# Two attention layers on one core: four key tiles per divisors' matmul, normalizations moved to ScalarE, elementwise work off GpSimd

## The chip, the cores and the metric

The kernel runs on one core of a Trainium2 chip. A core has five engines that work side by side and meet through semaphores: TensorE (matrix multiplication), VectorE and ScalarE (elementwise work), GpSimd (here elementwise work and the issue of some transfers) and SyncE (the issue of the other transfers). The metric is the device time of one execution in microseconds. The kernel before takes 3778.3 us, the median of three runs (3777.52 to 3778.91).

## The reference

The input `x` is four images of 256 channels and 64 x 64 pixels, all in fp32. Two layers follow each other, each of them `x = x + layer(groupnorm(x))` with 32 groups of 8 channels.

```python
# layer 0 ("A"): 8 heads of 32; queries from 4096 pixels, keys and values from a 2x2 strided convolution (1024)
q = einsum(Wq, x);  k = conv2x2(x, Wk);  v = conv2x2(x, Wv)
attn = softmax((q.k + q.(rel_h + rel_w)) * scale)        # 4096 x 1024 for each image and head
out = attn . v
# layer 1 ("B"): the 4096 pixels cut into 4 areas of 1024; attention inside each area
q, k, v = conv1x1(x, w_qkv) + b_qkv
attn = softmax(q.k * scale)                              # 1024 x 1024 for each image, area and head
out = attn . v + depthwise_conv7x7(v)
out = conv1x1(out, w_proj) + b_proj
```

In both layers each image has 8 chunks of 512 queries and two groups of four heads. The kernel calls one chunk with one group of four heads a **unit**: 16 units make a **block** (one layer of one image), and the eight blocks run in the order A0, A1, B0, A2, B1, A3, B2, B3 (layer and image). A unit goes over its 1024 keys in 8 **steps** of 128 keys.

## The kernel before

A unit's step `j` computes scores for four heads, exponentiates them without subtracting a maximum (a check at the end sends inputs with too large sums down another path), and multiplies the weights `p` of the step before with the values. `p` is a pair of tiles of 128 x 2 x 512, two heads each.

```python
def scores(unit, j):
    q, k = unit[1](), unit[2]()
    p = [pool.tile([P, 2, CH], FP, tag="p", name="p", bufs=10) for _ in range(2)]
    pairs = [ps_pair("s"), ps_pair("s")]
    for h in range(4):
        rows = slice(HD * h, HD * h + HD)
        T.matmul(pairs[h // 2][:, h % 2, :], lhsT=k[rows, j * P : (j + 1) * P], rhs=q[rows, :], ...)   # L213
    for i in range(2):
        S.activation(p[i], pairs[i], AF.Exp, scale=SCALE)                                              # L218
    return p

def weighted(unit, j, p, av):                        # av += v^T p, four matmuls, L225
    ...
```

The softmax's denominators are sums of `p` over all keys. They are made by a matmul with ones, and to halve those, the weights of two steps are added first: the first pair of heads by a transfer that accumulates (issued from GpSimd), the second by VectorE.

```python
def add_up(p, q):
    G.dma_start(p[0], q[0], accum_op=ALU.add)                                                          # L232
    V.tensor_add(p[1], p[1], q[1])                                                                     # L233

def divisors(g, n, p):
    ...
    for h in range(4):
        T.matmul(dens[g][HD * h : HD * h + HD, :], lhsT=ones[:, :HD],
                 rhs=p[h // 2][:, h % 2, :], start=(n == 0), stop=(n == NKT // 2 - 1))                 # L242
```

After a unit's last divisors, `divide` copies them to SBUF (L254), sends them through DRAM to spread them over the partitions, takes reciprocals (L259), broadcasts these back (`rb`) and multiplies (L266). The main loop, with the plan of side work in `do(g, j)`:

```python
while step < last or plan or later:
    g, j = divmod(step, NKT)
    if step < last:
        p = scores(units[g], j)
    do(g, j)
    if before is not None:
        weighted(*before)
        if j == 0:
            avs[g - 1] = pool.tile([P, CH], FP, tag="av", name="av_sb", bufs=2)
            S.copy(avs[g - 1], before[3])                                                              # L639
    if step < last:
        if j == 0:
            av = psum.tile([P, CH], FP, tag="av", name="av", bufs=1)
        if j % 2:
            add_up(before[2], p)
            later[step + 3] = g, j // 2, before[2]
    before = (units[g], j, p, av) if step < last else None
    if step in later:
        g, n, p = later.pop(step)
        divisors(g, n, p)
        if n == NKT // 2 - 1:
            divide(g, units[g])
    step += 1
```

The side work is placed by unit and step: projections for the next blocks (each a group of long matmuls with a copy on ScalarE), the normalizations

```python
def normalize(key, dst, src, t):
    mean, rstd = norms[key]
    V.tensor_scalar(dst, src, mean[:, t : t + 1], rstd[:, t : t + 1], ALU.subtract, ALU.mult)          # L194
```

of `taps` (256 elements a call, 128 calls), `hq` (512, 64 calls), `hv` (512, 64 calls) and `h` (1024, 32 calls), the residual adds on GpSimd (`add_residual`, L380, and `add_conv`, L484, each 32 times 128 x 1024), and the depthwise convolution, 49 taps for each of 32 pieces, on VectorE:

```python
            V.scalar_tensor_tensor(dst, src, w, dst, ALU.mult, ALU.add)                                # L578
    ...
    pace = 3.2                                 # units for one piece of the convolution
    start = max(start, ends[b] + 4.5)          # so it runs from about unit 20.5 to unit 126 of 128
```

Every engine works through its instructions in the order in which the program gives them.

Of the kernel before, what the change touches and what calls it, by code (L numbers as in the profile page):

```python
# [48 lines left out]
def direct_path(  # L49
# [109 lines left out]
    def plan_norm(key, g, j):  # L159
# [4 lines left out]
        def aggregate():  # L164
            for tag, cols in (("mv", 2), ("gmean", 1), ("dev", 1), ("gvar", 1), ("rstd", 1)):
                shape = [P, CT, cols] if cols > 1 else [P, CT]
                made[tag] = pool.tile(shape, FP, tag=tag, name=f"{tag}_{name}", bufs=3)
            norms[key] = made["gmean"], made["rstd"]
# [13 lines left out]
        def variances():  # L182
# [3 lines left out]
            G.tensor_tensor(made["rstd"], made["gvar"], neghalf, ALU.pow)  # L186

# [4 lines left out]
    def normalize(key, dst, src, t):  # L192
        mean, rstd = norms[key]
        V.tensor_scalar(dst, src, mean[:, t : t + 1], rstd[:, t : t + 1], ALU.subtract, ALU.mult)  # L194
# [12 lines left out]
    def scores(unit, j):  # L207
        q, k = unit[1](), unit[2]()
        p = [pool.tile([P, 2, CH], FP, tag="p", name="p", bufs=10) for _ in range(2)]
# [20 lines left out]
    def add_up(p, q):  # L230

        G.dma_start(p[0], q[0], accum_op=ALU.add)  # L232
        V.tensor_add(p[1], p[1], q[1])  # L233
# [3 lines left out]
    def divisors(g, n, p):  # L237
# [3 lines left out]
        for h in range(4):  # L241
            T.matmul(  # L242
                dens[g][HD * h : HD * h + HD, :], lhsT=ones[:, :HD],
                rhs=p[h // 2][:, h % 2, :], start=(n == 0), stop=(n == NKT // 2 - 1),
            )

    def divide(g, unit):
# [20 lines left out]
        at(g + 1, 6, reciprocals)  # L268
        at(g + 2, 1, multiply)

    def att_of(key):
        if key not in atts:
            atts[key] = pool.tile([P, CT, CH], FP, tag="att", name="att_" + "_".join(map(str, key)), bufs=2)
# [3 lines left out]
    def plan_a(b, u, prep):  # L277
# [101 lines left out]
        def add_residual(c):  # L379
            G.tensor_tensor(xcs[c], xcs[c], atts["A", b, c], ALU.add)  # L380
# [7 lines left out]
        for c in range(NCH):  # L388
# [4 lines left out]
            at(g + 2, 2, lambda c=c: load_residual(c))  # L393
            at(g + 3, 2, lambda c=c: add_residual(c))
            at(g + 3, 4, lambda c=c: store_chunk(c))
# [12 lines left out]
    def plan_b(b, u):  # L408
# [74 lines left out]
        def add_conv(c):  # L483
            G.tensor_tensor(rest[c][0], rest[c][0], atts["B", b, c], ALU.add)  # L484
# [18 lines left out]
        for c in range(NCH):  # L503
            g = u + 2 * c
            at(g + 2, 5, lambda c=c: load_rest(c))
            at(g + 3, 2, lambda c=c: add_conv(c))
            at(g + 3, 5, lambda c=c: project(c))
            at(g + 3, 7, lambda c=c: finish(c))
# [89 lines left out]
    for i, (layer, b) in enumerate(BLOCKS):  # L598
        u = i * UNITS
        if layer == "A":  # L600
            units += plan_a(b, u, u - UNITS)
            ends[b] = u + UNITS
            plan_norm(("B", b), u + UNITS + 1, 5)
# [4 lines left out]
    for b in range(B):  # L608
        start = max(start, ends[b] + 4.5)
# [20 lines left out]
    while step < last or plan or later:  # L630
# [9 lines left out]
        if step < last:  # L640
            if j == 0:
                av = psum.tile([P, CH], FP, tag="av", name="av", bufs=1)
            if j % 2:

                add_up(before[2], p)
                later[step + 3] = g, j // 2, before[2]
        before = (units[g], j, p, av) if step < last else None
        if step in later:
            g, n, p = later.pop(step)
            divisors(g, n, p)  # L650
# [609 lines left out]
```

## Time and profile before

| | us |
|---|---|
| device time, median of 3 | 3778.3 |
| span of the profiled execution | 3771.5 |
| TensorE matmuls busy | 3622.4 |
| VectorE busy | 2966.1 |
| ScalarE busy | 2365.4 |
| GpSimd busy | 639.7 |
| accumulating transfers, share of 16 engines' span | 38.2% |
| all other transfers of the SyncE queue, same measure | 21.1% |

A row of the profile's groups has the line of the kernel, the engine, the operation, the tiles it writes and reads with their shapes, the count, then the busy time in us and the mean length of one in ns, then the idle time of the engine just ahead of these instructions and what ended it. A matmul's end is modelled, so that neighbouring matmuls overlap in it. fp32 matmuls stand as two records each. In the timeline each row has the start in us, the length in us of the merged instructions, the engine, the line, the tiles and the count.

### The profile page before, as it was taken

Reading aid. Unit: us, or ns where it says so; the run is one execution under the profiler, and the core shown is the slowest. Engines: PE = TensorE matmul, PEld = TensorE weight load, DVE = VectorE, ACT = ScalarE, POOL = GpSimd, SP = SyncE. Lnnn points to the kernel's source line nnn. Section 1 sums busy time; section 2 is a strip of 40 time slices with the busy share of each in tenths; the row PEclk is TensorE's granted clock in tenths of the full one; section 3 lists DMA queues with packets and bytes.
Section 4 is the critical chain, followed back from the end, with each engine's and each line's share of the span. In section 5 each row is a group of like instructions: output and inputs, shape, how many; then the busy total and the mean of one; then the engine's idle time right before and its main releaser. Section 6 shows DMA issues by size and latency. Waiting matters only on the chain.

```text
span 3771.5 us, 57900 instructions
## 1 busy us (share of the span) xinstructions
PE 3622.4 (96%) x23330; PEld 1204.1 (32%) x23330; DVE 2966.1 (79%) x2972; ACT 2365.4 (63%) x2673; POOL 639.7 (17%) x600
## 2 busy tenths in 40 slices
PE   6999999999999999999999999999999999999996
PEld 5223432223332343222333234322233333333321
DVE  2333235999998878999998887899994689899992
ACT  1777466666666555666666665566666666666664
POOL 0122111111111111111111111111111111111111
PEclk9999999999999999999999999999999999999998
DMA  4666456666755655666675565566566556565554
GB/s 155 152 139 158 111 129 148 157 148 150 184 128 117 173 127 136 143 149 150 145 168 136 141 156 130 125 154 138 139 142 156 122 130 161 130 159 127 120 133 114
DMA packets 238790, 535.38 MB, mean 142 GB/s; under 512 B 62945, under 2 KB 69345, under 8 KB 238513
## 3 DMA queue, kind: packets, MB, share of 16 engines
q0 software_dynamic: 74080, 269.57, 38.2%
q1 hardware_dynamic: 163072, 259.61, 21.1%
q8 instruction: 184, 3.01, 0.3%
q10 hardware_dynamic: 1360, 2.43, 0.2%
q14 instruction: 94, 0.76, 0.1%
HBM read 193.85 MB, written 69.21 MB: 70 GB/s over the span
## 4 chain that ended last, share of the span: by engine, by line
PE 77%; DVE 11%; DMA 8%; issue 3%; ACT 1%; SPq 0%; POOL 0%; DVEq 0%; ACTq 0%; POOLq 0%
PE s L213 24%; PE av L225 20%; PE den L242 10%; DMA p<-p 6%; DVE acc L578 6%; PE k0ps L316 3%; PE v0ps L334 3%; PE ops L491 3%; PE v1ps L442 3%; PE k1ps L426 3%; PE vals_ps L538 3%; PE q1ps L453 3%; DVE p L233 2%; PE q0ps L370 2%; ACT p L218 1%
## 5 line engine op out<-in xcount | busy, mean ns | idle before, releaser
L218 ACT ACTIVATE p<-s 128x1024 f32<-128x1024 f32 x2048 | 1990.7, 1022 | 872.0 <-PE s L213 601.9
L578 DVE SCALAR_TENSOR_TENSOR acc<-vin,wpe_sb,acc 128x976 f32<-128x976 f32 (+14 forms) x1536 | 1950.4, 1270 | 35.2
L233 DVE TENSOR_TENSOR p<-p 128x1024 f32<-128x1024 f32 x512 | 633.0, 1236 | 577.3 <-PE av L225 271.0
L232 POOL DMA_DIRECT2D p<-p x512 | 440.3, 860 | 2930.0 <-ACT p L218 1133.1
L242 PE MATMUL den<-p,ones 128*32 128x512 f32 x4096 | 574.8, 599 | 73.4 <-DMA p<-p 61.7
L213 PE MATMUL s<-q,k_A 32*128 32x512 f32 x4096 | 626.9, 645 | 0.3 <-ACT p L218 0.3
L213 PE MATMUL s<-q,k_B 32*128 32x512 f32 x4096 | 615.0, 646 | 0.0
L225 PE MATMUL av<-p,v_B 128*32 128x512 f32 x4096 | 549.7, 608 | 0.4 <-ACT av_sb L639 0.3
L225 PE MATMUL av<-p,v_A 128*32 128x512 f32 x4096 | 548.5, 608 | 1.1 <-ACT av_sb L639 0.8
L213 PEld LDWEIGHTS s<-q,k_A 32*128 32x128 f32 x4096 | 197.9, 184 | 434.3 <-issue 219.2
L213 PEld LDWEIGHTS s<-q,k_B 32*128 32x128 f32 x4096 | 186.2, 184 | 435.1 <-issue 155.9
L242 PEld LDWEIGHTS den<-p,ones 128*32 128x32 f32 x4096 | 134.2, 110 | 422.2 <-issue 268.3
L225 PEld LDWEIGHTS av<-p,v_A 128*32 128x32 f32 x4096 | 80.8, 108 | 382.0 <-issue 342.7
L225 PEld LDWEIGHTS av<-p,v_B 128*32 128x32 f32 x4096 | 80.9, 108 | 363.2 <-issue 346.7
L491 PE MATMUL ops<-cv,wp_sb 128*128 128x512 f32 x256 | 119.9, 611 | 14.9 <-POOL cv L484 14.7
L538 PE MATMUL vals_ps<-hv,wqkv_sb 128*128 128x512 f32 x256 | 117.4, 607 | 7.7 <-ACT p L218 7.7
L316 PE MATMUL k0ps<-taps,wk_sb 128*128 128x256 f32 x512 | 119.6, 388 | 3.0 <-DVE taps L194 3.0
L442 PE MATMUL v1ps<-wqkv_sb,h 128*128 128x256 f32 x512 | 119.1, 386 | 0.0
L453 PE MATMUL q1ps<-h,wqkv_sb 128*128 128x512 f32 x256 | 118.4, 605 | 0.0
L426 PE MATMUL k1ps<-h,wqkv_sb 128*128 128x512 f32 x256 | 118.4, 605 | 0.0
L370 PE MATMUL q0ps<-hq,wq_sb 128*128 128x512 f32 x256 | 118.3, 605 | 0.0
L334 PE MATMUL v0ps<-wv_sb,taps 128*128 128x256 f32 x512 | 117.2, 383 | 0.0
(79 smaller groups left out, 1632.3 us busy)
## 6 DMA issues: line engine op xcount, KB each, us to landing
p<-p POOLq DMA_DIRECT2D x512, 512.0 KB, 5.2
rb<-recs SPq DMA_DIRECT2D x512, 64.0 KB
xs<-in_x SPq DMA_DIRECT2D x32, 512.0 KB
xa<-in_x SPq DMA_DIRECT2D x32, 512.0 KB
hq<-in_x SPq DMA_DIRECT2D x32, 512.0 KB
xc<-in_x SPq DMA_DIRECT2D x32, 512.0 KB
xmid<-xc SPq DMA_DIRECT2D x32, 512.0 KB
hv<-xmid SPq DMA_DIRECT2D x32, 512.0 KB
```

Source lines behind the costliest of these rows:

```text
L213: T.matmul(pairs[h // 2][:, h % 2, :], lhsT=k[rows, j * P : (j + 1) * P], rhs=q[rows, :], start=True, stop=True,)
L218: S.activation(p[i], pairs[i], AF.Exp, scale=SCALE)
L225: T.matmul(av[HD * h : HD * h + HD, :], lhsT=v[:, j, unit[0] * P + HD * h : unit[0] * P + HD * h + HD], rhs=p[h // 2][:, h % 2, :], start= ...
L232: G.dma_start(p[0], q[0], accum_op=ALU.add)
L233: V.tensor_add(p[1], p[1], q[1])
L242: T.matmul(dens[g][HD * h : HD * h + HD, :], lhsT=ones[:, :HD], rhs=p[h // 2][:, h % 2, :], start=(n == 0), stop=(n == NKT // 2 - 1),)
L316: T.matmul(ps, lhsT=wk0_sb[:, t, 2 * i + w, qd * P : (qd + 1) * P], rhs=taps[a][:, t, i, w], start=(n == 0), stop=(n == 7),)
L426: T.matmul(ps[:, half, :], lhsT=wqkv_sb[:, t, 1, qd * P : (qd + 1) * P], rhs=hs[a][:, t, half * CH : (half + 1) * CH], start=(t == 0), sto ...
L442: T.matmul(ps[:, m, :], lhsT=hs[a][:, t, kt * P : (kt + 1) * P], rhs=wqkv_sb[:, t, 2, :], start=(t == 0), stop=(t == CT - 1),)
L453: T.matmul(ps[:, qd, :], lhsT=wqkv_sb[:, t, 0, qd * P : (qd + 1) * P], rhs=hs[c // 2][:, t, (c % 2) * CH : (c % 2 + 1) * CH], start=(t == ...
L491: T.matmul(ps[:, to, :], lhsT=wp_sb[:, t, to * P : (to + 1) * P], rhs=cv[:, t, :], start=(t == 0), stop=(t == CT - 1),)
L578: V.scalar_tensor_tensor(dst, src, w, dst, ALU.mult, ALU.add)
```

## The change

Four steps' weights, not two, are added up before one group of divisors' matmuls, which halves the number of those groups from 512 to 256. For that, VectorE adds the second pair's tiles three times in four steps, and the transfers of the first pair form a small tree: steps 1 into 0 and 3 into 2, and three steps later 2 into 0. The weights stay longer, so there are 13 buffers of `p` for 10, and one buffer of `att` for two. The divisors now stand in steps 1 and 5, after the weighted sum; before, they stood in every even step.

VectorE hands the normalizations to ScalarE, as one activation with a scale and a shift per channel (`shift = -mean * rstd`, made by two small operations on GpSimd), and takes over the residual adds from GpSimd, which is left with issuing transfers, apart from these small operations. The other edits move side work to fit: reciprocals, multiplications, residual adds and projections later, the convolution 0.4 unit later.

```diff
--- before.py
+++ after.py
@@ -162,10 +162,10 @@
         made = {}
 
         def aggregate():
-            for tag, cols in (("mv", 2), ("gmean", 1), ("dev", 1), ("gvar", 1), ("rstd", 1)):
+            for tag, cols in (("mv", 2), ("gmean", 1), ("dev", 1), ("gvar", 1), ("rstd", 1), ("shift", 1)):
                 shape = [P, CT, cols] if cols > 1 else [P, CT]
                 made[tag] = pool.tile(shape, FP, tag=tag, name=f"{tag}_{name}", bufs=3)
-            norms[key] = made["gmean"], made["rstd"]
+            norms[key] = made["shift"], made["rstd"]
             mv = made["mv"]
             for t in range(CT):
                 V.bn_aggr(out=mv[:, t, :], in_=stats[key][:, t].rearrange("p c s -> p (c s)"))
@@ -184,14 +184,16 @@
             T.matmul(ps, lhsT=gmat, rhs=made["dev"], start=True, stop=True)
             S.activation(made["gvar"], ps, AF.Identity, bias=eps)
             G.tensor_tensor(made["rstd"], made["gvar"], neghalf, ALU.pow)
+            G.tensor_tensor(made["shift"], made["gmean"], made["rstd"], ALU.mult)
+            G.tensor_scalar(made["shift"], made["shift"], -1.0, None, ALU.mult)
 
         at(g, j, aggregate)
         at(g, j + 1, means)
         at(g, j + 3, variances)
 
     def normalize(key, dst, src, t):
-        mean, rstd = norms[key]
-        V.tensor_scalar(dst, src, mean[:, t : t + 1], rstd[:, t : t + 1], ALU.subtract, ALU.mult)
+        shift, rstd = norms[key]
+        S.activation(dst, src, AF.Identity, bias=shift[:, t : t + 1], scale=rstd[:, t : t + 1])
 
 
     qs, ks, vs, atts = {}, {}, {}, {}
@@ -206,7 +208,7 @@
 
     def scores(unit, j):
         q, k = unit[1](), unit[2]()
-        p = [pool.tile([P, 2, CH], FP, tag="p", name="p", bufs=10) for _ in range(2)]
+        p = [pool.tile([P, 2, CH], FP, tag="p", name="p", bufs=13) for _ in range(2)]
         pairs = [ps_pair("s"), ps_pair("s")]
         for h in range(4):
             rows = slice(HD * h, HD * h + HD)
@@ -227,10 +229,12 @@
                 rhs=p[h // 2][:, h % 2, :], start=(j == 0), stop=(j == NKT - 1),
             )
 
-    def add_up(p, q):
-
-        G.dma_start(p[0], q[0], accum_op=ALU.add)
-        V.tensor_add(p[1], p[1], q[1])
+    def add_up(j, p, q, p4):
+
+        if j % 2:
+            G.dma_start(q[0], p[0], accum_op=ALU.add)
+        if j % 4:
+            V.tensor_add(p4[1], p4[1], p[1])
 
     dens, avs = {}, {}
 
@@ -241,7 +245,7 @@
         for h in range(4):
             T.matmul(
                 dens[g][HD * h : HD * h + HD, :], lhsT=ones[:, :HD],
-                rhs=p[h // 2][:, h % 2, :], start=(n == 0), stop=(n == NKT // 2 - 1),
+                rhs=p[h // 2][:, h % 2, :], start=(n == 0), stop=(n == NKT // 4 - 1),
             )
 
     def divide(g, unit):
@@ -265,12 +269,12 @@
         def multiply():
             V.tensor_mul(unit[4]()[:, unit[0], :], avs.pop(g), rb)
 
-        at(g + 1, 6, reciprocals)
-        at(g + 2, 1, multiply)
+        at(g + 2, 0, reciprocals)
+        at(g + 2, 3, multiply)
 
     def att_of(key):
         if key not in atts:
-            atts[key] = pool.tile([P, CT, CH], FP, tag="att", name="att_" + "_".join(map(str, key)), bufs=2)
+            atts[key] = pool.tile([P, CT, CH], FP, tag="att", name="att_" + "_".join(map(str, key)), bufs=1)
         return atts[key]
 
 
@@ -377,7 +381,7 @@
             xcs[c] = load_chunk(b, c, "xc")
 
         def add_residual(c):
-            G.tensor_tensor(xcs[c], xcs[c], atts["A", b, c], ALU.add)
+            V.tensor_add(xcs[c], xcs[c], atts["A", b, c])
 
         def store_chunk(c):
             xc = xcs.pop(c)
@@ -390,9 +394,9 @@
             at(g - 2, 4, lambda c=c: fetch(c))
             at(g - 1, 1, lambda c=c: norm_chunk(c))
             at(g - 1, 4, lambda c=c: make_q(c))
-            at(g + 2, 2, lambda c=c: load_residual(c))
-            at(g + 3, 2, lambda c=c: add_residual(c))
-            at(g + 3, 4, lambda c=c: store_chunk(c))
+            at(g + 2, 4, lambda c=c: load_residual(c))
+            at(g + 3, 4, lambda c=c: add_residual(c))
+            at(g + 3, 5, lambda c=c: store_chunk(c))
         return [
             (
                 n % 2,
@@ -481,7 +485,7 @@
             rest[c] = cv, xm
 
         def add_conv(c):
-            G.tensor_tensor(rest[c][0], rest[c][0], atts["B", b, c], ALU.add)
+            V.tensor_add(rest[c][0], rest[c][0], atts["B", b, c])
 
         def project(c):
             cv, xm = rest[c]
@@ -502,10 +506,10 @@
 
         for c in range(NCH):
             g = u + 2 * c
-            at(g + 2, 5, lambda c=c: load_rest(c))
-            at(g + 3, 2, lambda c=c: add_conv(c))
-            at(g + 3, 5, lambda c=c: project(c))
-            at(g + 3, 7, lambda c=c: finish(c))
+            at(g + 3, 0, lambda c=c: load_rest(c))
+            at(g + 3, 4, lambda c=c: add_conv(c))
+            at(g + 3, 7, lambda c=c: project(c))
+            at(g + 4, 1, lambda c=c: finish(c))
         return [
             (
                 n % 2,
@@ -600,13 +604,13 @@
         if layer == "A":
             units += plan_a(b, u, u - UNITS)
             ends[b] = u + UNITS
-            plan_norm(("B", b), u + UNITS + 1, 5)
+            plan_norm(("B", b), u + UNITS + 1, 7)
         else:
             units += plan_b(b, u)
     pace = 3.2
     start = 0.0
     for b in range(B):
-        start = max(start, ends[b] + 4.5)
+        start = max(start, ends[b] + 4.9)
         for c in range(NCH):
             plan_values(b, c, start - 2.4 + max(0, c - 2) * pace)
         for a in range(NAREA):
@@ -640,16 +644,22 @@
         if step < last:
             if j == 0:
                 av = psum.tile([P, CH], FP, tag="av", name="av", bufs=1)
-            if j % 2:
-
-                add_up(before[2], p)
-                later[step + 3] = g, j // 2, before[2]
+
+            if j % 4 == 0:
+                four = p
+            elif j % 4 == 1:
+                later.setdefault(step + 8, []).append(lambda g=g, n=j // 4, p=four: divisors(g, n, p))
+            elif j % 4 == 3:
+                later.setdefault(step + 3, []).append(
+                    lambda p=four, q=before[2]: G.dma_start(p[0], q[0], accum_op=ALU.add)
+                )
+            if j:
+                add_up(j, p, before[2], four)
+            if j == NKT - 1:
+                later.setdefault(step + 6, []).append(lambda g=g: divide(g, units[g]))
         before = (units[g], j, p, av) if step < last else None
-        if step in later:
-            g, n, p = later.pop(step)
-            divisors(g, n, p)
-            if n == NKT // 2 - 1:
-                divide(g, units[g])
+        for f in later.pop(step, []):
+            f()
         step += 1
```

## Prediction

> **What bounds the kernel now.** I read the page first (busy shares, groups, queues), then the timeline of a few steps, then busy time block by block, then the waits. From the page:
>
> ```profile
> PE 3622.4 (96%) x23330; PEld 1204.1 (32%) x23330; DVE 2966.1 (79%) x2972; ACT 2365.4 (63%) x2673; POOL 639.7 (17%) x600
> ...
> L578 DVE SCALAR_TENSOR_TENSOR acc<-vin,wpe_sb,acc 128x976 f32<-128x976 f32 (+14 forms) x1536 | 1950.4, 1270 | 35.2
> L233 DVE TENSOR_TENSOR p<-p 128x1024 f32<-128x1024 f32 x512 | 633.0, 1236 | 577.3 <-PE av L225 271.0
> L232 POOL DMA_DIRECT2D p<-p x512 | 440.3, 860 | 2930.0 <-ACT p L218 1133.1
> L242 PE MATMUL den<-p,ones 128*32 128x512 f32 x4096 | 574.8, 599 | 73.4 <-DMA p<-p 61.7
> ```
>
> Taken alone this says that TensorE is the limit and that halving the 574.8 us of `den` matmuls pays 287 us. Two further views say otherwise. A matmul's busy time overlaps its neighbours', so the price of a divisors' group is read from the starts of the score matmuls, in the first A block (no convolution beside it):
>
> ```profile
> 249.79 0.59 ACT L639 COPY av_sb<-av 128x512 f32<-128x512 f32 x1
> 249.84 1.14 PE L213 MATMUL s<-q,k_A 32*128 32x512 f32 x8
> ...
> 251.91 1.31 PE L213 MATMUL s<-q,k_A 32*128 32x512 f32 x8
> ...
> 254.04 1.04 PE L242 MATMUL den<-p,ones 128*32 128x512 f32 x8
> 255.01 1.14 PE L213 MATMUL s<-q,k_A 32*128 32x512 f32 x8
> ...
> 257.07 1.31 PE L213 MATMUL s<-q,k_A 32*128 32x512 f32 x8
> ```
>
> A step of scores and weighted sum alone takes 2.07 us (249.84 to 251.91, 255.01 to 257.07); with divisors 3.10. A group costs 1.03 us. A unit of eight steps is 8 x 2.07 + 4 x 1.03 = 20.7 us, plus about 3.63 us for each projection of eight long matmul records (its steps last 5.70).
>
> Busy time by block (A0, A1, B0, A2, B1, A3, B2, B3, cut at each block's first score matmul; columns: stretch, length, then PE, PEld, DVE, ACT and POOL busy, clock, DMA share, GB/s):
>
> ```profile
> 91.00:507.00 416.00, 414.78 (x2863) 143.97 (x2862) 135.30 (x194) 277.83 (x313) 74.45 (x71) 1.00 0.60 134
> ...
> 931.00:1441.00 510.00, 502.30 (x3132) 186.05 (x3128) 443.68 (x449) 309.32 (x361) 79.68 (x74) 1.00 0.59 142
> 1441.00:1869.00 428.00, 408.18 (x2723) 115.30 (x2718) 414.18 (x389) 283.88 (x312) 78.75 (x72) 0.99 0.64 149
> ...
> 2391.00:2813.00 422.00, 403.92 (x2700) 112.20 (x2696) 411.90 (x386) 280.87 (x306) 80.65 (x72) 0.99 0.63 146
> ```
>
> In A0 VectorE is a third busy: TensorE's block. In A2 and A3 VectorE is busy 414 of 428 and 412 of 422 us, and the rest is largely turnaround between instructions, while TensorE's own floor by the step prices above is only about 393 and 385. There the depthwise convolution on VectorE is the bound, and TensorE waits for it through `den` and the weight buffers. The B blocks carry more projections (floor about 507 in B0) and are TensorE's again. So the kernel alternates between two bounds.
>
> What GpSimd's adds cost is seen in the timeline:
>
> ```profile
> 2018.02 5.14 DVE L578 SCALAR_TENSOR_TENSOR acc<-vin,wpe_sb,acc 128x976 f32<-128x976 f32 x4
> ...
> 2025.16 2.70 POOL L484 TENSOR_TENSOR cv<-cv,att_B 128x1024 f32<-128x1024 f32 x1
> 2025.37 4.85 DVE L578 SCALAR_TENSOR_TENSOR acc<-vin,wpe_sb,acc 128x1008 f32<-128x1008 f32 x2
> ```
>
> Four taps alone take 5.14 us, two beside a GpSimd add 4.85: one add costs VectorE about 2.1 to 2.3 us. DMA issues on GpSimd show no such effect: taps beside them keep their length.
>
> **What the Trainium skill says.** "SBUF — State Buffer", section "Who interferes with whom": a VectorE instruction with two SBUF inputs contends with a GpSimd instruction that reads SBUF. The trace agrees (the lines above). "VectorE: DVE Perf Modes", section "The perf-mode tier table": in fp32 an add of two tensors runs at single rate, a one-source tensor-scalar operation at double. It agrees: 1.22 us for an add of 1024, 0.54 for a normalization of 512. So VectorE gives away its cheapest operations and gets dear ones. "ScalarE: Activation LUTs", section "What ACT_TABLE_LOAD costs": 186 ns + 0.833 ns per element, 93 ns for each per-partition operand, 93 ns overlapped back to back. The trace has 683 ns for 512 with one such operand; the page's sum is 706. "DMA: Bandwidth & Descriptors", section "SWDGE vs HWDGE vs iDMA": accumulating transfers can be issued only from GpSimd, so the added ones join the same queue. Here that queue has all 512.
>
> **The change part by part.**
>
> *Divisors.* 512 groups become 256: 256 x 1.03 = 264 us of TensorE, 33 per block, where TensorE is the limit. Some comes back. (a) With no divisors in step 0, the next score matmul ends about 1 us earlier, but the copy of `av` (0.59 us) still follows the step's exp pair (1.94 us), and the next unit's first weighted sum needs that copy: about 0.5 us per unit, 8 per block. (b) Several bare steps in a row are paced by ScalarE: 1.94 plus a gap of 0.18 us is 2.12 against 2.07, about 2 per block. (c) Normalizations, below, about 4. Net 33 - 14 = 19 per block.
>
> *Adds on VectorE.* `p4[1] += p[1]` in three steps of four instead of two: 256 more, 1.14 us from start to start, 292 us. 64 residual and convolution adds come from GpSimd: 73 us.
>
> *Taken from VectorE.* Normalizations, start to start: 128 x 0.32 + 128 x 0.46 + 32 x 0.72 = 123 us; about 54 collisions with GpSimd adds x 2.1 = 113 us. An add placed between two dependent taps also spares about 0.11 us of turnaround, about 28 us. Net + 292 + 73 - 123 - 113 - 28 = + 101 us.
>
> *For A2 alone*: 32 adds + 36.5, eight residual adds + 9.1, collisions - 16.8, normalizations - 16 (16 of `hq`, about 10 of `hv`, 6 of `h`), turnarounds - 4: + 9 on a stage that VectorE already fills. Its few idle microseconds take some: + 5.
>
> *ScalarE.* By the page's figures 128 x 0.49 + 128 x 0.71 + 32 x 1.13, an estimate of 190 us, to about 2,555 in all. Most `hq` normalizations fall in step 1 and taps in step 5, where the divisors now stand and exp has a microsecond to spare; I charge a quarter where TensorE is the limit, nothing where VectorE is.
>
> *Transfers.* 768 accumulations instead of 512: that queue's 38.2% of the span becomes 57%, the whole 59% becomes about 79%, more in the A blocks. The last one of a group of four has three steps until its divisors, as before (median landing 5.2 us); in A0's short steps two in a row could make it late. Thirteen buffers give four steps before reuse, where before the odd step's had three, which helps.
>
> *Ends.* The last unit has one more transfer in its chain (+ 5), the start two tiny GpSimd operations and slower taps (+ 3), the last add is faster on VectorE (- 2): + 6.
>
> **The sum**, block by block: A0 - 14 (19 less some late transfers); A1 - 8 (half of it has the convolution); B0 - 5 and B1 - 8 (TensorE's 19, but units without projections are VectorE's: 30 us of VectorE against about 26); A2 + 5; A3 + 8 (it had less idle time hidden in it); B2 - 18; B3 0 (VectorE's sum rises to about 413, TensorE's falls to about 415). That is - 40; ends + 6; transfer pressure + 5: - 29. 3778 - 29 = 3749, say 3750.
>
> **Rivals.** (1) TensorE stays the bound throughout and the change brings nearly all of 264 us: about 3,530. For it: 96% busy on the page. Against it: A2's VectorE. A milder form, in which the deeper buffers let VectorE's surplus in one unit run into the slack of the next, would give about 3,680. (2) ScalarE becomes the pace: normalizations delay exp, exp delays the next weighted sum, and all 190 us land on the path where TensorE leads: about 100 of them there, 3,840. For it: exp already paces bare steps. Against it: the places chosen for them. (3) The accumulating queue falls behind: `den` waits for transfers (61.7 us now) double or triple: 3,800 to 3,850. Against it: 79% is not full, and the chain has slack in the long steps.
>
> **Range and chances.** The gain on TensorE and the loss on VectorE are both sure; how they mix within a block is not, and that decides between some - 90 and + 60. So 3,685 to 3,815 for 8 in 10. Faster by over 2% (below 3,703) needs the milder form of the first rival: 0.2. Slower by over 2% (above 3,854) needs two of the pressures at once: 0.08. Within 2%: 0.72.
>
> **What would show it.** VectorE busy near 3,070 us and about 98% in A1's second half, A2 and A3, whose lengths stay at 425 to 440 us; A0 and B2 shorter by 10 to 20; steps with divisors still about 3.1 and bare ones about 2.1; a wait of weighted sums for `av_sb` of about 0.5 us per unit; ScalarE near 2,555; the accumulating queue near 57%. A2 and A3 below 410 us would prove the VectorE bound wrong; `den` waiting for transfers over 200 us would make it rival 3; exp waiting for normalizations, rival 2.

## The result, and the profile after

The changed kernel takes 3905.06 us (median of 4, 3897.21 to 3908.96) where the kernel before took 3777.91. The ratio is 1.0335, with a 95% interval of 1.0315 to 1.0355: slower by 127 us, where 28 us less was predicted. The range (3685 to 3815) does not hold it.

From the page of the kernel after, the lines that answer to those of before:

```profile
PE 3564.0 (91%) x21282; PEld 1188.4 (30%) x21282; DVE 3076.9 (79%) x3004; ACT 2538.0 (65%) x2961; POOL 690.2 (18%) x808
...
q0 software_dynamic: 110944, 403.81, 55.1%
...
L582 DVE SCALAR_TENSOR_TENSOR acc<-vin,wpe_sb,acc 128x976 f32<-128x976 f32 (+14 forms) x1536 | 1881.0, 1225 | 28.8
L237 DVE TENSOR_TENSOR p<-p 128x1024 f32<-128x1024 f32 x768 | 936.5, 1220 | 472.5 <-ACT p L220 271.8
...
L246 PE MATMUL den<-p,ones 128*32 128x512 f32 x2048 | 277.8, 615 | 88.1 <-DMA p<-p 87.9
```

Nearly everything that the prediction counted is here: half the divisors' matmuls, 256 more adds, VectorE at 3,077 us, ScalarE at 2,538, the accumulating queue at 55%. (The queue's row has its packets, its MB and the time that they took as a share of the 16 DMA engines' span.) But TensorE's share fell from 96% to 91% although its busy time hardly fell: the kernel waits more, and each matmul takes a little longer (615 ns against 599 for the divisors).

Where it waits does not stand in the `den` row. Block by block, A0 and A2 of the kernel after (columns as in the table of blocks of before):

```profile
93.00:522.00 429.00, 410.81 (x2609) 140.85 (x2607) 163.21 (x186) 302.34 (x361) 83.87 (x97) 0.97 0.78 166
...
1501.00:1946.00 445.00, 400.65 (x2468) 112.16 (x2472) 422.29 (x399) 302.79 (x341) 83.49 (x96) 0.96 0.81 181
```

A0 was to lose 14 us and gained 13. In A2 VectorE is busy 422 of 445 us, where it was 414 of 428: it is still nearly full, but has 23 us of idle time instead of 14. The DMA share has gone from 0.60 to 0.78 in A0 and from 0.64 to 0.81 in A2, and the clock has fallen.

VectorE's own waits grew with it. Kernel before (total us, times, longest):

```profile
DVE att_A L266 <- DMA rb<-recs: 50.1, 16, 5.2
DVE att_B L266 <- DMA rb<-recs: 49.3, 17, 7.0
...
DVE few L259 <- DMA few<-rows: 3.9, 1, 3.9
```

Kernel after:

```profile
DVE att_B L270 <- DMA rb<-recs: 90.2, 29, 10.6
DVE att_A L270 <- DMA rb<-recs: 73.2, 25, 7.6
DVE few L263 <- DMA few<-rows: 61.2, 27, 9.8
```

`few` and `rb` are the small round trips of the divisors through DRAM: `den_sb` to `rows`, `rows` to `few`, reciprocals to `recs`, `recs` to `rb`. In all VectorE stood still for them for 103.3 us before and for 224.6 us after. These transfers are small and are not on the accumulating queue, but that queue now carries 134 MB more (403.81 against 269.57), on the same DMA engines; whether this is what makes them late is put to the test below. An instruction that VectorE has reached blocks everything behind it, so a convolution with no interest in `rb` waits with it.

The total must be read by block. In the order A0, A1, B0, A2, B1, A3, B2, B3 the waits are 74, 27, 13, 12, 16, 17, 20 and 46 us, where they were 37, 11, 4, 1, 7, 1, 13 and 30. So over half of them lie in A0 and B3. In A0 VectorE is busy only 163 of 429 us and can afford to wait. In A2 and A3, which VectorE fills, they rose by 27 us together; there the second-level transfers (the 2-into-0 ones) cost 32 us together, as the table of blocks below shows.

SyncE, which issues the round trips, waits for `rows` to be written 128 times in each kernel. Kernel before, kernel after, and the change without its second-level transfers (the run comes below):

```profile
SPq L256 <- DMA rows<-den_sb: 216.6, 128, 5.3
...
SPq L260 <- DMA rows<-den_sb: 491.9, 128, 13.5
...
SPq L260 <- DMA rows<-den_sb: 419.7, 128, 8.9
```

Most of this rise, then, comes with other parts of the change and not with the added transfers.

A second new wait stands on TensorE: scores waiting for exp. Before and after:

```profile
PE s L213 <- ACT p L218: 0.3, 1, 0.3
...
PE s L215 <- ACT p L220: 98.5, 42, 12.9
```

One such place in the trace, at 820 us, ScalarE and TensorE only:

```profile
820.27 1.14 PE L215 MATMUL s<-q,k_A 32*128 32x512 f32 x8
...
822.34 1.13 PE L215 MATMUL s<-q,k_A 32*128 32x512 f32 x4
...
830.14 1.52 ACT L196 ACTIVATE hq<-hq,shift_A,rstd_A 128x512 f32<-128x512 f32 x2 [9.94 <-DMA hq<-in_x]
831.57 1.91 ACT L220 ACTIVATE p<-s 128x1024 f32<-128x1024 f32 x2
...
832.62 2.08 PE L215 MATMUL s<-q,k_A 32*128 32x512 f32 x4 [9.16 <-ACT p L220]
```

The normalization of `hq` now stands in ScalarE's line ahead of the exp. Its load was late, so ScalarE waits 9.94 us, and TensorE 9.16 us for the exp behind it. Why the load was late stands in SyncE's line, which issues loads and round trips in one order:

```profile
804.69 0.32 SPq L265 DMA_DIRECT2D recs<-few  x1
...
815.64 0.54 SPq L89 DMA_DIRECT2D hq<-in_x  x1
```

Between the two stand the wait for `recs`, four issues of `rb`, and the loads of `h`, `vin` and `xc`, all in one line; the load of `hq` left at 815.64 and its data came some 14 us later.

The same place shows a third thing. The four records of score matmuls at 822.34 took 1.13 us, those at 832.62 took 2.08. The stretches of the timeline with the granted clock as the last column but two:

```profile
820.00:823.00 3.00, 3.00 (x24) 0.77 (x20) 2.96 (x4) 0.21 (x1) 0.86 (x1) 1.00 1.04 267
...
832.00:835.50 3.50, 2.88 (x11) 0.70 (x12) 3.25 (x5) 3.50 (x4) 0.00 (x0) 0.50 0.07 21
835.50:839.00 3.50, 3.50 (x17) 1.00 (x10) 3.46 (x4) 2.44 (x4) 0.86 (x1) 0.50 0.84 242
```

After the gap TensorE runs at half its clock. There are 17 such stretches in the kernel before, 86.7 us in all, and 50 in the kernel after, 311.3 us in all. TensorE's gaps of more than 0.25 us add up to 106.9 us before and 301.1 after.

### The profile page after: what moved, and what is told of

Same layout as the page of the kernel before. It is cut to its first block, busy times and chain, and to the rows that moved or that the text cites. A ratio compares the mean times of both kernels' runs of the same rounds, so it can differ in the third digit from the quotient of the medians.

```text
span 3907.2 us, 54882 instructions
## 1 busy us (share of the span) xinstructions
PE 3564.0 (91%) x21282; PEld 1188.4 (30%) x21282; DVE 3076.9 (79%) x3004; ACT 2538.0 (65%) x2961; POOL 690.2 (18%) x808
## 3 DMA queue, kind: packets, MB, share of 16 engines
q0 software_dynamic: 110944, 403.81, 55.1%
## 4 chain that ended last, share of the span: by engine, by line
PE 50%; DVE 26%; DMA 14%; issue 5%; ACT 3%; SPq 2%; POOL 0%; DVEq 0%; ACTq 0%; POOLq 0%
PE s L215 15%; DVE acc L582 15%; PE av L227 12%; DVE p L237 7%; DMA p<-p 6%; DMA recs<-few 3%; PE den L246 3%; PE v0ps L338 3%; PE k0ps L320 3%; PE ops L495 2%; DMA rb<-recs 2%; PE vals_ps L542 2%; PE v1ps L446 2%; PE q1ps L457 2%; PE k1ps L430 2%
## 5 line engine op out<-in xcount | busy, mean ns | idle before, releaser
L582 DVE SCALAR_TENSOR_TENSOR acc<-vin,wpe_sb,acc 128x976 f32<-128x976 f32 (+14 forms) x1536 | 1881.0, 1225 | 28.8
L237 DVE TENSOR_TENSOR p<-p 128x1024 f32<-128x1024 f32 x768 | 936.5, 1220 | 472.5 <-ACT p L220 271.8
L235 POOL DMA_DIRECT2D p<-p x512 | 442.2, 864 | 2959.4 <-ACT p L220 1203.3
L215 PE MATMUL s<-q,k_A 32*128 32x512 f32 x4096 | 673.9, 654 | 53.3 <-ACT p L220 52.8
L215 PE MATMUL s<-q,k_B 32*128 32x512 f32 x4096 | 665.3, 654 | 45.8 <-ACT p L220 45.8
L227 PE MATMUL av<-p,v_A 128*32 128x512 f32 x4096 | 594.2, 614 | 41.9 <-ACT p L220 31.7
L215 PEld LDWEIGHTS s<-q,k_B 32*128 32x128 f32 x4096 | 207.1, 187 | 507.8 <-issue 289.4
L246 PE MATMUL den<-p,ones 128*32 128x512 f32 x2048 | 277.8, 615 | 88.1 <-DMA p<-p 87.9
L654 POOL DMA_DIRECT2D p<-p x256 | 273.0, 1066 | 179.0 <-DMA p<-p 86.5
L495 PE MATMUL ops<-cv,wp_sb 128*128 128x512 f32 x256 | 131.1, 660 | 26.2 <-DVE cv L488 26.2
L246 PEld LDWEIGHTS den<-p,ones 128*32 128x32 f32 x2048 | 62.8, 111 | 255.2 <-DMA p<-p 131.8
```

The source lines that it names most:

```text
L227: T.matmul(av[HD * h : HD * h + HD, :], lhsT=v[:, j, unit[0] * P + HD * h : unit[0] * P + HD * h + HD], rhs=p[h // 2][:, h % 2, :], start= ...
L235: G.dma_start(q[0], p[0], accum_op=ALU.add)
L237: V.tensor_add(p4[1], p4[1], p[1])
L495: T.matmul(ps[:, to, :], lhsT=wp_sb[:, t, to * P : (to + 1) * P], rhs=cv[:, t, :], start=(t == 0), stop=(t == CT - 1),)
L654: lambda p=four, q=before[2]: G.dma_start(p[0], q[0], accum_op=ALU.add)
```

## The experiments

Theories: **(T)** the 256 added transfers slow the small ones, and the engines stand in line for these; **(S)** normalizations in ScalarE's line delay exp; **(D)** the divisors themselves wait for the last transfer of a group of four; **(V)** VectorE's added work is the cost. All ratios are to the kernel before on the same chip, with 95% intervals.

### Undoing one part of the change at a time

Normalizations back on VectorE:

```diff
-        S.activation(dst, src, AF.Identity, bias=shift[:, t : t + 1], scale=rstd[:, t : t + 1])
+        V.tensor_scalar(dst, src, rstd[:, t : t + 1], shift[:, t : t + 1], ALU.mult, ALU.add)
```

> The changed kernel (3,905 us) with its normalizations put back on VectorE, all else as changed. ScalarE theory (a normalization in ScalarE's line holds the exps behind it, by its length or because its own load is late, TensorE runs dry and then runs at half clock): about 3,800 us, score matmuls waiting for exps in single long gaps vanish, half-clock stretches fall from 50 to about 30. Transfer theory (the 256 second-level accumulations make divisors and loads late): about 3,890, the long waits of den stay near 88 us. VectorE theory (its 101 us more are the loss): 123 us go back to VectorE, about 3,960.

Measured 3864.64 us, ratio 1.0226 [1.0209, 1.0243]: 40 us back, between the ScalarE and the transfer theory. TensorE's wait for exp is almost gone, as the waits of this kernel show:

```profile
PE s L215 <- ACT p L220: 6.4, 5, 3.1
```

VectorE's wait for round trips stays (238.9 us).

The second-level transfer left out. The denominators of the first pair of heads then lack half of their terms; everything else is computed:

```diff
-                    lambda p=four, q=before[2]: G.dma_start(p[0], q[0], accum_op=ALU.add)
+                    lambda p=four, q=before[2]: None
```

> The changed kernel with the second-level accumulating transfer of each group of four left out (the first pair of heads' denominators then lack half of their terms; nothing else is left out). Transfer theory: the waits of den for transfers go from 88 us to under 20, loads come earlier, about 3,780 us. ScalarE theory: only the den waits go, about 3,860. VectorE theory: 3,900, unchanged.

Measured 3777.71, ratio 0.9999 [0.9990, 1.0008]: 127 us back, the whole loss. VectorE's wait for round trips falls to 60.9 us, below that of before:

```profile
DVE att_B L270 <- DMA rb<-recs: 28.5, 9, 7.3
DVE att_A L270 <- DMA rb<-recs: 23.2, 15, 4.0
DVE few L263 <- DMA few<-rows: 9.2, 9, 2.2
```

A2 of this kernel:

```profile
1446.00:1876.00 430.00, 403.91 (x2466) 113.66 (x2464) 420.18 (x398) 302.17 (x340) 54.98 (x64) 0.97 0.63 149
```

VectorE is busy 420 of 430 us: with the transfers gone, A2 is full again, and at the length that was predicted for it.

Both together:

> The changed kernel with both: normalizations on VectorE and the second-level transfers left out. If ScalarE's line and the transfers are the two separate causes, their savings add: about 3,680 to 3,700 us. If one hides behind the other, no better than the better of the two runs alone. VectorE theory: about 3,900 or more, since VectorE then carries some 3,190 us of work.

Measured 3745.66, ratio 0.9915 [0.9898, 0.9932], above the expected 3,680 to 3,700. As measured, the two parts nearly add up: 40 + 127 = 167, together 159. So the change without the second-level traffic and without ScalarE's normalizations would gain 32 us. (V) falls as the cause of the loss: VectorE's sum of three adds in four, the residual adds and, here, the normalizations as well are all in this kernel.

### Waiting for the transfer, or sharing the engines with it

The transfer kept, same 512 KB at the same place, but it adds its source to itself, so that no divisors wait for it (the first pair again lacks half of its terms):

```diff
-                    lambda p=four, q=before[2]: G.dma_start(p[0], q[0], accum_op=ALU.add)
+                    lambda p=four, q=before[2]: G.dma_start(q[0], q[0], accum_op=ALU.add)
```

> The changed kernel, where the second-level transfer still moves the same 512 KB at the same place but adds its source tile to itself, so that no divisors' matmul waits for it (the first pair's denominators lack half of their terms). The traffic stays, the wait goes. If the loss is the wait of the divisors for a transfer issued too shortly before (latency): about 3,780 us, as without the transfer. If the loss is the load on the transfer engines (everything else lands later): about 3,890. Between the two: shares.

Measured 3885.05, ratio 1.0283 [1.0266, 1.0300]. Of the 127 us only 20 are the divisors' waiting (D); 107 remain with a transfer for which no divisors wait. VectorE's wait for round trips is 262.1 us:

```profile
DVE few L263 <- DMA few<-rows: 90.3, 30, 8.3
DVE att_A L270 <- DMA rb<-recs: 87.4, 25, 8.6
DVE att_B L270 <- DMA rb<-recs: 84.4, 31, 10.2
```

These transfers do one thing more than load the engines: they hold tiles of `p`, and exp waits for a free tile. Exp's waits that end with such a transfer, in the kernel after, in this kernel and without the second-level transfers:

```profile
ACT p L220 <- DMA p<-p: 139.6, 69, 5.7
...
ACT p L220 <- DMA p<-p: 131.9, 70, 5.7
...
ACT p L220 <- DMA p<-p: 9.6, 9, 2.7
```

No run takes these waits away and leaves the traffic of the changed kernel, so their share of the 107 us is open.

Divisors two steps later, with all that follows from them, so that the transfers have more time (the first of the edits are shown; the division, the residual adds, the stores and the output projection move with them):

```diff
-                later.setdefault(step + 8, []).append(lambda g=g, n=j // 4, p=four: divisors(g, n, p))
+                later.setdefault(step + 10, []).append(lambda g=g, n=j // 4, p=four: divisors(g, n, p))
...
-        at(g + 2, 0, reciprocals)
-        at(g + 2, 3, multiply)
+        at(g + 2, 2, reciprocals)
+        at(g + 2, 5, multiply)
```

> The changed kernel with the divisors' matmuls two steps later (10 instead of 8 steps after the group's second), and what follows on them two steps later too; same buffers, same work. Latency theory: the waits of den for transfers fall from 88 us to under 20 and most of 127 us comes back, about 3,800. Load theory: the loads for ScalarE's normalizations are as late as before, about 3,880. A rival of its own: the group's first tiles stay two steps longer in the 13 buffers, exps wait for a free one, slower than 3,905.

Measured 3951.24, ratio 1.0452 [1.0431, 1.0474]: 46 us slower still. TensorE's wait of `den` for transfers fell to 4.3 us, and others took its place: 90.9 us of weighted sums waiting for `av_sb` (13.4 in the kernel after), 103.6 us of scores waiting for exp, while exp itself waited 215.6 us for VectorE's adds (96.3 in the kernel after). The buffers of `p` and `av_sb` are held two steps longer, and there are no more of them. (D) is refuted as the main cause, and more distance is not free.

### One part of the change put into the kernel before

Normalizations on ScalarE alone:

```diff
-        V.tensor_scalar(dst, src, mean[:, t : t + 1], rstd[:, t : t + 1], ALU.subtract, ALU.mult)
+        S.activation(dst, src, AF.Identity, bias=shift[:, t : t + 1], scale=rstd[:, t : t + 1])
```

> The kernel before (3,778 us) with its normalizations on ScalarE and nothing else changed (VectorE loses 123 us). ScalarE theory: slower, about 3,840 us, with new gaps of score matmuls that end with a normalization. Transfer theory: the transfers are as before, so about 3,765. VectorE theory: faster, about 3,740, since the A blocks are VectorE's.

Measured 3826.09, ratio 1.0127 [1.0110, 1.0143]: 48 us slower, with no transfer added. The normalizations on ScalarE cost something by themselves.

The residual and convolution adds on VectorE alone:

```diff
-            G.tensor_tensor(xcs[c], xcs[c], atts["A", b, c], ALU.add)
+            V.tensor_add(xcs[c], xcs[c], atts["A", b, c])
...
-            G.tensor_tensor(rest[c][0], rest[c][0], atts["B", b, c], ALU.add)
+            V.tensor_add(rest[c][0], rest[c][0], atts["B", b, c])
```

> The kernel before (3,778 us) with the residual adds on VectorE alone. By VectorE's sum (64 adds, + 73 us, against 54 collisions, - 113 us) the A2 and A3 blocks, which VectorE fills, get about 8 us shorter each: 3,755 to 3,765 us. If collisions cost nothing on the path: 3,778 or, with 73 us more on VectorE, up to 3,800.

Measured 3752.54, ratio 0.9936 [0.9919, 0.9952]: 26 us faster. This part of the change is a gain: VectorE pays for the adds and is spared the collisions.

Both of these parts:

> The kernel before with normalizations on ScalarE and residual adds on VectorE, pairs as before: the change without the summing of four. If the parts add: 3,778 + 48 - 26 = 3,800 us. If ScalarE's line (the 48 us) gets cheaper or dearer once VectorE is quicker, below 3,790 or above 3,810.

Measured 3811.30, ratio 1.0090 [1.0070, 1.0111]: 33 us slower, where the parts added, 48 - 26, would give 22.

The sum of four alone, that is the kernel after with the normalizations on VectorE and the adds on GpSimd:

> The changed kernel with the normalizations back on VectorE and the residual adds back on GpSimd: the summing of four alone, with its places. Against the run with only the normalizations back (3,865 us) VectorE gets some 113 us of collisions and loses 73 us of adds. VectorE theory: about 20 us slower than that run, 3,885. Transfer theory: no difference, 3,865. If the adds on VectorE were a loss in themselves: faster, about 3,845.

Measured 3908.33, ratio 1.0351 [1.0334, 1.0368]: + 130, and 44 us above the run with only the normalizations back, where 20 at most had been expected. The adds on VectorE are thus a gain here too, and a larger one. The three parts measured singly, 130 + 48 - 26 = 152, are 25 us more than the 127 of the whole: they add up only roughly.

### The traffic by itself

The kernel before with 256 extra accumulating transfers of 512 KB that no divisors wait for (13 buffers for `p`, as in the kernel after):

```diff
+            if j % 4 == 3:
+                extra[step + 3] = p[0]
...
+        if step in extra:
+            q0 = extra.pop(step)
+            G.dma_start(q0, q0, accum_op=ALU.add)
```

> The kernel before, and in each group of four steps one more accumulating transfer of 512 KB, of a tile of weights that is no longer needed onto itself (256 in all, nobody waits for their result; 13 buffers of p and one of att so that the tile may stay longer). Load theory: the traffic alone costs what the second-level transfers cost in the changed kernel, some 100 us: 3,870 to 3,890. If the loss needs the changed kernel's order or its ScalarE normalizations: under 3,800.

Measured 3834.72, ratio 1.0143 [1.0126, 1.0160]: slower by 56 us, where 3,870 to 3,890 was expected. VectorE's wait for round trips rises from 103.3 to 224.6 us, as in the kernel after, and so the traffic alone makes the small transfers late:

```profile
DVE att_B L266 <- DMA rb<-recs: 115.0, 28, 12.4
DVE att_A L266 <- DMA rb<-recs: 102.9, 35, 5.8
DVE few L259 <- DMA few<-rows: 6.7, 3, 5.6
```

The price is about half of the 107 us of the changed kernel. Of exp's waits the profile names none here that ends with a transfer, but it leaves 168.0 us of them without a cause (3.4 us in the kernel after).

That the 13 buffers are not what costs was seen from the kernel before with the adds on VectorE and 13 buffers (and one for `att`):

> The kernel before with residual adds on VectorE, 13 buffers of p for 10 and one of att for two, nothing else: what the buffers alone do. If exps waiting for a free buffer (153.6 us by the waits of the kernel before, for transfers) are on the path in the A blocks: some 10 to 20 us under 3,753. If they only reflect VectorE's pace: 3,753.

Measured 3747.89, ratio 0.9921 [0.9904, 0.9938], against 3752.54 with 10: no loss. Exp's waits that end with a transfer went from 134.4 us to none, and the kernel became at most these 5 us faster, so here they were hardly on the path.

### Taking VectorE out of the line

If (T) acts through VectorE standing in line, later places for its two readers should give most of the 107 us back. Reciprocals two steps later, the multiply three steps later, and its followers two or three (the first of them are shown):

```diff
-        at(g + 2, 0, reciprocals)
-        at(g + 2, 3, multiply)
+        at(g + 2, 2, reciprocals)
+        at(g + 2, 6, multiply)
...
-            at(g + 3, 4, lambda c=c: add_residual(c))
-            at(g + 3, 5, lambda c=c: store_chunk(c))
+            at(g + 3, 7, lambda c=c: add_residual(c))
+            at(g + 4, 0, lambda c=c: store_chunk(c))
```

> The changed kernel with the reciprocals two steps later, the multiplication by them three, and what follows on them (residual adds, stores, output projection) two to three steps later; the divisors stay where they are, so the small transfers few and rb get five and four steps for three and three. Theory of VectorE's line (the second-level traffic slows few and rb, VectorE stands in line for them, 225 us against 61 without that traffic, in blocks that VectorE fills): these waits fall under 90 us and half or more of the traffic's 107 us comes back, 3,830 to 3,860. If the traffic does its harm through den and ScalarE's late loads: 3,890 to 3,905.

Measured 3863.56, ratio 1.0223 [1.0203, 1.0242]: 41 us back, less than the half that was asked for. The waits moved as meant, and a new one appeared. VectorE's waits of this kernel:

```profile
DVE att_B L270 <- DMA rb<-recs: 28.7, 12, 6.9
...
DVE few L263 <- DMA few<-rows: 12.4, 6, 5.0
...
DVE att_A L270 <- DMA rb<-recs: 5.8, 7, 2.1
```

and TensorE's first:

```profile
PE av L227 <- ACT av_sb L643: 112.7, 62, 6.7
```

VectorE's 224.6 us have become 46.9. But the multiply is what frees `av_sb`, of which there are two, and the next unit's weighted sum now waits for one: 112.7 us, where it was 13.4 in the kernel after. A third `av_sb` was not tried.

By block the run says more. In A0 VectorE's wait fell from 74 to 4 us and `av_sb` brought no new one (2.3 and 2.9 us), yet the block takes 428 us as before: there VectorE's standing in line cost nothing, although the second-level transfers cost A0 19 us (table below). A2 waits 33 us for `av_sb` and is 7 us longer. What came back lies mostly in B0 and B2, 16 and 17 us. VectorE's line may account for the loss in A2 and A3; it does not in A0.

The same with the normalizations back on VectorE:

> The same with the normalizations back on VectorE (3,865 us without the later places). VectorE's line: its waits for few and rb fall from 239 us to under 90, 3,790 to 3,820. Otherwise 3,850 to 3,865.

Measured 3841.13, ratio 1.0161 [1.0139, 1.0183], between the two expectations. A further 22 us, but still 95 us above the kernel with neither normalizations on ScalarE nor second-level transfers (3745.66).

### Sums of four only where VectorE is idle, and with no transfer

The runs say what to keep: the adds on VectorE, the sum of four where it costs no transfer. In A0 VectorE is a third busy. The kernel before with the adds on VectorE, and in its first 20 units both pairs summed over four tiles by VectorE alone:

```diff
-            if j % 2:
+            if g in FOURS:
+                if j % 4 == 0:
+                    four = p
+                else:
+                    V.tensor_add(four[0], four[0], p[0])
+                    V.tensor_add(four[1], four[1], p[1])
+                if j % 4 == 3:
+                    later[step + 3] = g, j // 4, four
+            elif j % 2:
```

> An attempt at a better kernel: the one before with residual adds on VectorE (3,753 us), where in the first 20 units, which have no convolution, four tiles of both pairs are summed by VectorE alone, with no transfer of weights; 13 buffers of p, one of att. By the prediction's own price (2.06 us less per unit, 0.5 back for the copy of av) 20 x 1.5 = 30 us: 3,723. VectorE theory: it is a third busy there, so no loss; if bare steps are ScalarE's, less, 3,735.

Measured 3712.87, ratio 0.9823 [0.9805, 0.9841]. Against the same kernel without sums of four (3747.89) that is 35 us for 40 groups of divisors saved, 0.88 us each; a group had been priced at 1.03. The 80 transfers of these units are gone as well (the DMA share of A0 is 0.18 instead of 0.60), and what that gave was not separated.

With units 98, 99, 126 and 127 added:

```diff
-    FOURS = set(range(20))
+    FOURS = set(range(20)) | {98, 99, 126, 127}
```

> The better kernel (3,713 us: residual adds on VectorE, fours summed by VectorE in the first 20 units) with units 98, 99, 126 and 127, which have no convolution either, summed in fours too. By 1.5 to 2 us per unit: 3,705 to 3,708; if VectorE's work of the neighbouring units spills into them: 3,713.

Measured 3703.08, ratio 0.9807 [0.9790, 0.9825]: the fastest, ahead of both kernels, though its interval overlaps that of the run just above. Its page:

```profile
PE 3568.9 (96%) x22946; PEld 1190.2 (32%) x22946; DVE 3136.5 (85%) x3228; ACT 2364.6 (64%) x2673; POOL 370.0 (10%) x440
```

VectorE does still more here than in the kernel after (3,137 us against 3,077), and TensorE is back at 96%. Half-clock stretches are down to 10, 56 us in all.

## Why the prediction was wrong

**The step that failed is "transfer pressure + 5".** It was written beside a correct count: 57% was predicted for the accumulating queue and 55.1% measured; 79% was predicted for the whole, and 78 to 82% measured in the A blocks. The error was to ask only who waits for the added transfers: the divisors, and these had slack. Their waiting cost 20 us (the transfer that adds to itself). The other 107 us come with the transfers although no divisors wait for them. That the traffic makes other, small transfers late is shown (VectorE's waits for these go from 103.3 to 224.6 us by traffic alone); how the 107 us divide among their readers, exp's waits for tiles and the clock is not. Rival 3 came close, but with the wrong sign to look for: "`den` waiting for transfers over 200 us". It is 87.9. The range was built from how TensorE's gain and VectorE's loss mix, and this term had no share in it.

**A second step was mis-sized: ScalarE, "I charge a quarter where TensorE is the limit", about 4 us per block.** Measured by block (us from the block's first score matmul to the next block's, for B3 to its last score matmul, as differences from the kernel before; "norms moved alone" is the kernel before with only the normalizations on ScalarE, "and norms back" the change with neither second-level transfers nor normalizations on ScalarE):

| block | predicted | norms moved alone | no 2nd-level transfers | and norms back | the change |
|---|---|---|---|---|---|
| A0 | - 14 | + 11.8 | - 6.1 | - 21.5 | + 12.7 |
| A1 | - 8 | + 4.0 | - 10.8 | - 7.3 | + 13.5 |
| B0 | - 5 | + 8.7 | + 18.9 | + 3.4 | + 30.6 |
| A2 | + 5 | - 3.5 | + 3.1 | + 14.5 | + 17.7 |
| B1 | - 8 | + 12.8 | + 13.6 | - 12.3 | + 16.4 |
| A3 | + 8 | - 2.5 | + 8.7 | + 15.9 | + 25.6 |
| B2 | - 18 | + 14.7 | - 15.3 | - 19.4 | + 4.5 |
| B3 | 0 | + 3.4 | - 13.8 | - 6.5 | + 6.1 |

"Nothing where VectorE is" was right: A2 and A3 even get shorter. But where TensorE leads (A0, B0, B1, B2) the moved normalizations cost 9 to 15 us per block, not 4. In that kernel the divisors stand in other steps than the prediction's charge assumed; in the changed kernel's places ("no 2nd-level transfers" against "and norms back") they cost 15, 16, 26 and 4 us. Their own length had been judged well: ScalarE's busy time rose by 173 us, against an estimate of 190. Why they cost more than a quarter of it is not shown. In the changed kernel they also carry their loads' lateness into exp's line, as at 820 us: ScalarE waits 47 us for loads ahead of a normalization. In the kernel with the normalizations alone that is 2.1 us, and scores wait for exp only 30.6 us, and still it is 48 us slower.

**What held.** With the two terms taken out, the sum is as predicted in kind and nearly in size: without second-level transfers A0, A1, A2 and A3 are within 8 us of the predicted and B2 within 3, and with the normalizations back the whole gains 32 us, where 40 had been summed over the blocks. That last nearness is partly luck: A2 and A3 are 10 and 8 us longer than predicted there, A0 8 us shorter. B3 came out 14 us better than the 0 it was given. A2 and A3, predicted at 425 to 440 us and VectorE's, are 430.2 and 430.8 without second-level transfers (444.8 and 447.7 with them). VectorE's sum was + 101 and is + 111. The step prices held: in A0 without second-level transfers most bare steps take 2.07 to 2.24 us, step 5 with divisors 2.92 to 3.10. The charge for `av_sb`, 0.5 us per unit, held as well: step 1, whose weighted sum waits for that copy, takes 3.43 us, although TensorE's waits for `av_sb` come to only 13.4 us in the whole kernel after. B0 and B1 were wrong even without the second-level transfers, by 24 and 22 us; with the normalizations back B1 is right to 4 us and B0 to 8, so most of it is the ScalarE term.

**The rivals.** The first (TensorE's whole 264 us) is out. The second (exp waits) and the third (transfers) came together: 40 and 127 us. The 0.08 for "slower" was argued as "needs two of the pressures at once". That was wrong too: the change without its ScalarE part stands at 3864.64, over the 3,854 of the limit, so one pressure was enough.

**What stays open.** The traffic costs 107 us in the changed kernel and 56 in the kernel before, with 262.1 us of VectorE's waiting in the first and 224.6 in the second. Later readers took most of VectorE's waits away and gave 41 us back before the buffers of `av_sb` became the new wait; whether more would follow with a third buffer was not tried, and in A0 nothing followed though no new wait appeared. Exp's wait for tiles that transfers hold (131.9 us in the changed kernel) is a rival that was not tested by itself there. A part may be the clock. An estimate: TensorE was busy at half clock for 214 us in the kernel after and for 173 without the second-level transfers; at half the work, that is 107 against 86 us, 21 of the 127. No run held the clock while the waits stayed, and where VectorE leads, a slower TensorE need cost nothing. So this is argued, not shown.

## What to carry to other kernels

Price an added transfer by what it does to the smallest transfers that anyone waits for, not only by its own reader: look for the round trips, for the engine whose line they stand in, and for the buffers that a later reader would hold. Moving work to an engine that is a third idle is not free when its place in the line is ahead of something that is on the path: here it cost 48 us with loads that were 2.1 us late in all, and a late load holds up everything behind it, as at 820 us. When one part of a change saves work and another pays for it in a shared resource, do the saving only in the stages where the payer is idle: here 48 groups of divisors saved by VectorE alone gave 45 us, with fewer transfers than before, where 256 saved by way of added transfers went with a loss of 127.

## What the runs showed of the hardware

The Trainium skill, "TensorE: Matmul & The Clock Gate", section "Part 1: The HAM clock gate (the "warmup" mystery)", says that the array falls to half its clock after at least one idle window of about 3.4 us. That length shows in the slow stretches: all but the last of each kernel last 3.41 us or a multiple of it. As the idle time that is needed it doesn't hold: in the kernel before, 12 of the 15 gaps of 2 to 3 us in TensorE's work are followed by such a stretch. Of all gaps of 2 us or more, 37 of 42 in the kernel after and 16 of 19 in the kernel before are, and of gaps of 1 to 1.9 us 6 of 41 and 0 of 20. Yet 2 us is no threshold: 13 of the 50 stretches in the kernel after follow shorter gaps alone, down to 0.9 us. A stretch of 3.41 us holds back 1.7 us of full clock at most (an estimate, half its length), and 22 of the 50 are longer.

Second, how unevenly a loaded set of DMA engines slows its users. With the traffic alone added to the kernel before, the 512 KB accumulations' median landing went from 5.2 to 6.1 us, by a sixth, while SyncE's wait for the small write of `rows` went from 1.7 to 3.1 us on average (216.6 and 393.0 us over 128), by four fifths.

Third, moving 64 adds off GpSimd to a VectorE that is busy four fifths of the time makes the kernel 26 us faster: the collisions cost more than the adds. They fall on normalizations as well: in the kernel before, one of `h` takes 0.80 us alone and up to 2.87 us beside a GpSimd add.
